# A decoder layer in exact fp32: one projection earlier, the experts' loads between the small transfers, a held piece and one tile's experts later

## The chip, the cores and the metric

The kernel runs on one core of a Trainium2 chip. A core has five engines that run side by side: TensorE (PE: matrix products and transposes, into PSUM), VectorE (DVE), ScalarE (ACT), GpSimd (POOL), and SyncE (SP), which here only issues transfers. The engines work through their own instructions in order and wait for each other through semaphores. Transfers between the chip's memory (HBM) and the core's SBUF are carried out by 16 DMA engines. The metric is the device time of one execution in microseconds (us); lower is better.

## The reference

Sixteen sequences of 128 tokens with 256 features go through one layer of three parts, each followed by "add the input and normalize":

```python
# 1. causal attention, 16 heads of 16, only the 32 largest scores of each row are kept
scores = jnp.einsum('bhqd,bhkd->bhqk', q, k) / math.sqrt(D_HEAD)
scores = jnp.where(causal, neg_inf, scores)
vals, idx = jax.lax.top_k(scores, K_S)                       # K_S = 32
attn = jax.nn.softmax(masked, axis=-1)
x = _layernorm(x + (attn @ v) @ Wo.T + bo)
# 2. eight experts on every token (256 -> 512 -> 256), summed with weights from ctx_512 and itok
h = jax.nn.relu(jnp.einsum('edi,bsi->bsed', proj_in, x))
o = jnp.einsum('eid,bsed->bsei', proj_out, h)
x = _layernorm(x + jnp.einsum('bsei,bse->bsi', o, gate))
# 3. Hadamard transform, 4-bit activations, ternary weights
x = _layernorm(x + jnp.einsum('bsi,oi->bso', xq, wq))
```

All weights and activations of parts 1 and 2 are fp32.

## The kernel before

The 16 sequences form nine tiles of 1, 1, 2, 2, 2, 2, 2, 2 and 2 sequences. Attention works in units: a unit is one tile, one half of the heads (c = 0 or 1) and one sequence. Tiles 0 and 1 have two units each (units 0, 1 and 2, 3), every other tile four.

The engines that compute follow an order written out by hand. One step of the loop `attention()` is one round of VectorE's work on one unit; a unit has STEPS = 9 steps (four rounds of "find the eight largest", L440, and "strike them out", L455, in all). `attn_finish` then ends the softmax: z (L467), its reciprocal (L469), products on VectorE (L471) and POOL (L475). A dictionary `plan`, filled with `at(step, fn, ...)`, says which other function is traced at which step. The functions that matter here:

- `project(u)`: queries and keys of one half of a tile (`queries_keys`, L331). ScalarE writes them from PSUM into qT (L347) and kT (L352). Eight small transfers on SyncE's queue (L365) then spread qT over the block-diagonal buffer qblk. qT comes from a pool with two buffers; a third qT can be written only when the eight transfers of the first have read it. The PSUM tiles of these projections come from the pool psh with two buffers, which the held pieces (L285) and the experts' first product (ph, L618) use too.
- `carry(t)`: values (L375) and the residual.
- `score(u)`: the score products (L396); for units after the first, ScalarE copies them to SBUF (L405).
- `attn_turn` (the transposes pta and ptb, L486 and L487, evacuated by ScalarE as pT, L496), `attn_apply` (pav, L507), `attn_end` (py, L520, then VectorE's r, L523, and the normalization to x1) and the transposes px (L535) of x1 to x1T (L536).
- `hoist()`: projections of the last three tiles (6, 7, 8) done early in nine pieces and parked in HBM; until then their inputs and results occupy the places of experts 5, 6 and 7 in SBUF. In the row `for step in (8, 10, 12, 15, 16, 17, 17, 21, 22)` two pieces stand at step 17.
- `load_experts(es)`: two transfers of 512 KB for each expert, on SyncE's queue. They are traced inside `project`, for experts 0 to 2 behind the eight transfers of (t, c) = (2, 0), and for 3 and 4 behind those of (3, 0), where the constant `hada` follows.

The experts (`experts`, L618 and L585, evacuated by ScalarE as hT, L622, and part, L593) and the third part (`ffn`) fill TensorE between attention's products. `pace(step)` says how much of this work must have been traced by a step: the work of tile t is spread evenly from `begin[t]` to `begin[t + 1]`. `begin` is 23, 50, 84 and 120 for the first four tiles. x tiles come from a pool with three buffers, so the x of tile 3 takes over the buffer of tile 0, which r of tile 0 (L523) reads last.

TensorE, VectorE, ScalarE and GpSimd keep the order in which the code is traced. SyncE's transfers are ordered by the scheduler of the language, which keeps them behind what they depend on.

Of the kernel before, what the change touches and what calls it, by code (L numbers as in the profile page):

```python
# [29 lines left out]
def decoder_kernel(ctx: ExitStack, tc: tile.TileContext, i: dict, out: bass.AP):  # L30
# [6 lines left out]
    NT = len(SIZES)  # L37
# [3 lines left out]
    FIRST_UNITS = DC * SIZES[0]  # L41
# [40 lines left out]
    def load_x(t):  # L82
        x = b3.tile([P, TB, D], F32, tag="x", name=f"x{t}")
        nc.sync.dma_start(x[:, : SIZES[t]], i["x"][tokens(t), :].rearrange("(b p) d -> p b d", p=P))
        return x

    def load(t, q):
        return load_T(t, q), load_x(t)

    def load_gates(t):  # L90
        n, bs = SIZES[t], slice(FIRST[t], FIRST[t] + SIZES[t])
        w = b3.tile([P, TB, S], F32, tag="ctx", name=f"ctx{t}")
        nc.sync.dma_start(w[:, :n], i["ctx_512"][bs].rearrange("b k s -> k b s"))
        k = b3.tile([P, TB, S], I32, tag="tok", name=f"tok{t}")
        nc.sync.dma_start(k[:, :n], i["itok"][bs].rearrange("b k s -> k b s"))
        return w, k
# [29 lines left out]
    FIRST_HELD = E - len(HOISTED)  # L126
# [18 lines left out]
    def load_experts(es):  # L145
        for e in es:
            nc.sync.dma_start(w_in[:, e], i["w_in"][e].rearrange("(c p) d -> p c d", p=P))
            nc.sync.dma_start(w_out[:, e], i["w_out"][e].rearrange("(c p) d -> p c d", p=P))
# [127 lines left out]
    def hoist():  # L276

        for t in HOISTED:
            e = place(t)
            xT = w_in[:, e, :, :T]  # L280
            for c in range(DC):
                pp = psh.tile([P, 2, T], F32, tag="ph", name=f"phq{t}_{c}")
                for j, w in enumerate((wqT, wkT)):
                    for cc in range(DC):
                        nc.tensor.matmul(pp[:, j], w[:, cc, ts(c, P)], xT[:, cc], start=cc == 0, stop=cc == DC - 1)  # L285
                for j, bias in enumerate((bq, bk)):
                    nc.scalar.activation(w_out[:, e, 2 * j + c], pp[:, j], AF.Identity, bias=bias[:, c : c + 1])
                if c == DC - 1:
                    qk_held = dram.tile([P, 2, DC, T], F32, name=f"qk_held{t}")
                    nc.sync.dma_start(qk_held.rearrange("p j c s -> p (j c) s"), w_out[:, e])  # L290
                yield
            pv = pso.tile([P, 512], F32, tag="po", name=f"phv{t}").rearrange("p (b d) -> p b d", b=TB)
            for b in range(TB):
                for c in range(DC):
                    nc.tensor.matmul(pv[:, b], xT[:, c, ts(b, S)], wvT[:, c], start=c == 0, stop=c == DC - 1)  # L295
            nc.scalar.copy(w_in[:, e, :, T:], pv)
            v_held = dram.tile([P, TB, D], F32, name=f"v_held{t}")
            held[t] = qk_held, v_held, nc.sync.dma_start(v_held, w_in[:, e, :, T:])
            yield

    def held_queries_keys(t, c):

        n, src = SIZES[t], held[t][0]
        kT = kTs[(t * DC + c) % len(kTs)]
        qblk = qblks[(t * DC + c + 2) % len(qblks)]
        for g in range(2):
            rows = ts(g, 64)
            nc.sync.dma_start(kT[rows, :, g], src[rows, 1, c].rearrange("p (b s) -> p b s", b=n))
        for h in range(HC):
            ins = nc.sync.dma_start(  # L310
                qblk[ts(h, DH), :, :, h % HG].rearrange("p b m q -> p (b m) q"),
                src[ts(h, DH), 0, c].rearrange("p (m q) -> p m q", q=32),
            )
        return qblk, kT, ins
# [507 lines left out]
    def project(u):  # L822

        if u >= len(units) or units[u][:2] in projected:
            return
        t, c, _ = units[u]
        projected.append((t, c))
        *qk[t, c], ins = held_queries_keys(t, c) if t in HOISTED else queries_keys(t, c, inputs[t][0])
        if c == 0 and 2 < t < NT - 1:
            inputs[t + 1] = (None, load_x(t + 1)) if t + 1 in HOISTED else load(t + 1, nc.sync)  # L830
        if (t, c) in ((2, 0), (3, 0)):
            with tc.issue_after(ins.ins):
                load_experts(range(3) if t == 2 else range(3, FIRST_HELD))
                if t == 3:
                    nc.sync.dma_start(hada, i["hada"][0:P, 0:P])
        if (t, c) == (1, DC - 1):
            gate_inputs[1] = load_gates(1)
# [18 lines left out]
    STEPS = 2 * (TOPK // 8) + 1  # L856
    LAG = 1
    LAST = [DC * sum(SIZES[: t + 1]) - 1 for t in range(NT)]
# [5 lines left out]
    def at(step, fn, *args):  # L864
        plan.setdefault(step, []).append(lambda: fn(*args))
# [25 lines left out]
    for u, (t, c, b) in enumerate(units):  # L891
        s, quick = STEPS * (u + 1), u < FIRST_UNITS
        if (c, b) == (0, 0):
            at(s - STEPS, open_tile, t)
        if u in lag:
            at(s + lag[u], attn_finish, u)
        late = lag.get(u, 0)
        turn = s + (0 if quick else late + 2 if u == LAST[2] else late + 3 if u in lag else 1 if t < 3 else 3)
        at(turn, attn_turn, u)
        at(turn + 2, products, u)  # L900
        if u == LAST[t]:
            for k in (2, 3, 4, 4) if quick else (4, 6, 10, 11) if t == 1 else (6, 8, 10, 11):
                at(s + k, end, t)
            for k in (-3, -1, *range(5, 5 + E)) if quick else (-5, -3, *range(9, 9 + E)):
                at(s + k, next_of_gates, t)
            at(s - 1, next_gates, t + 2)
    for u in range(len(units) - 1):
        at(STEPS * u + (5 if u == FIRST_UNITS else 1), score, u + 1)
    for step, u in ((3, 2), (5, 3), (7, 4), (STEPS + 3, 6), (2 * STEPS + 3, 8)):
        at(step, project, u)  # L910
    for step, t in ((3, 1), (7, 2), (2 * STEPS + 5, 3)):
        at(step, carry, t)
    for u in range(FIRST_UNITS + 1, len(units)):
        at(STEPS * u + 5, project, u + 6)
        if u + 6 < len(units) and units[u + 6][1:] == (0, 0):
            at(STEPS * u + 7, carry, units[u + 6][0])
    for step, zs in ((1, [odd(vms[2]), odd(vms[3])]), (6, [pTs[1], odd(vms[4]), odd(vms[5])])):
        at(step, zeros_later, zs)
    hoisting = hoist()
    for step in (8, 10, 12, 15, 16, 17, 17, 21, 22):  # L920
        at(step, next, hoisting)

    def load_held_experts():
# [6 lines left out]
    for step in (38, 40, 47, 49, 56):  # L930
        at(step, next, weights_of_last)

    begin = [STEPS * (LAST[t] + 1) + (5, 14, 12)[t] if t < 3 else STEPS * (LAST[t] + 1) + 12 for t in range(NT)]

    def attention():
        project(0)
        score(0)
        project(1)
        carry(0)
        inputs[3] = load(3, nc.sync)  # L940
        for u in range(len(units)):
            yield from attn_weights(u, scores.pop(u))
        for _ in range(begin[-1] - STEPS * len(units)):
            yield
# [31 lines left out]
    for step, _ in enumerate(attention()):  # L976
        for fn in plan.get(step, ()):
            fn()
        while done < pace(step):
            c = next(work)  # L980
# [48 lines left out]
```

## Time and profile before

| | us |
|---|---|
| median of 3 runs | 621.82 (621.14 to 622.28) |
| the profiled execution's own time | 622.15 |
| its span, first to last instruction | 620.4 |
| TensorE busy | 599.4 (97%) |
| VectorE busy | 508.6 (82%) |
| ScalarE busy | 339.3 (55%) |
| POOL busy | 303.0 (49%) |
| 16 small transfers of 8 KB on SyncE's queue, issue to landing, median | 1.8 |
| qk and v held transfers, 512 and 256 KB, median | 8.3 and 3.3 |
| expert loads of 512 KB, median (w_in, w_out) | 6.9 and 8.0 |

The granted clock of TensorE was full (0.994 on average), so differences are not due to the clock. In the lines shown below, a group of a timeline gives its start, its length (both us), engine, line, operation, output and inputs, count, and in square brackets the idle time of its engine just before it with what ended that; a wait list gives the sum of waits, their number and the longest. Where the engine named as the releaser had long been done, it was another thing, often a transfer. The time from issue to landing of a transfer is in the view of transfers, which can be narrowed to one issue.

### The profile page before, as it was taken

What the parts mean: (1) busy time and instruction counts of PE and PEld (TensorE: products, weight loads), DVE (VectorE), ACT (ScalarE), POOL (GpSimd) and SP (SyncE); (2) the same over time, 40 slices, a digit from 0 to 9 for tenths busy, and PEclk for the clock granted to TensorE, in tenths of its full rate; (3) what the DMA queues carried; (4) which work ended last, traced back from release to release, by engine and by line L of the source; (5) the groups of instructions that cost most, each with busy time, mean ns of one, the idle gap of its engine ahead of it and who ended that gap; (6) DMA issues with size and microseconds to landing.
All of it is one profiled execution on the core that took longest, in us unless ns stands there. A gap on an engine that the chain in (4) does not pass through costs nothing.

```text
span 620.4 us, 12489 instructions
## 1 busy us (share of the span) xinstructions
PE 599.4 (97%) x3534; PEld 522.4 (84%) x3534; DVE 508.6 (82%) x3132; ACT 339.3 (55%) x1016; POOL 303.0 (49%) x574
## 2 busy tenths in 40 slices
PE   6989999999999999999999999999999999999993
PEld 5779898988888888888888888888888888888882
DVE  6978999989967999889979997899969996431346
ACT  3867667665666565556565655546565655341112
POOL 6204553412883438623883468443772368227013
PEclk9999999999999999999999999999999999999997
DMA  7184940010002100130003000000000000000000
GB/s 239 38 260 141 323 111 6 23 27 8 11 19 38 40 19 2 29 57 3 17 18 52 18 10 1 1 18 1 2 1 1 18 10 2 0 18 1 0 18 17
DMA packets 53589, 25.13 MB, mean 40 GB/s; under 512 B 31888, under 2 KB 51088, under 8 KB 53520
## 3 DMA queue, kind: packets, MB, share of 16 engines
q1 hardware_dynamic: 52960, 24.20, 14.3%
q8 instruction: 28, 0.46, 0.3%
q14 instruction: 41, 0.34, 0.2%
q10 hardware_dynamic: 560, 0.13, 0.1%
HBM read 18.68 MB, written 4.46 MB: 37 GB/s over the span
## 4 chain that ended last, share of the span: by engine, by line
PE 89%; DVE 5%; ACT 4%; issue 1%; POOL 1%; DMA 0%; ACTq 0%; DVEq 0%
PE po L585 34%; PE ph L618 34%; PE ps L396 5%; PE pav L507 3%; PE pqk L331 3%; PE py L520 2%; PE pta L486 2%; PE phq L285 1%; DVE wk L455 1%; ACT ex L431 1%; DVE m L440 1%; PE pv L375 1%; PE phv L295 1%; ACT pT L496 1%; PE ptb L487 1%
## 5 line engine op out<-in xcount | busy, mean ns | idle before, releaser
L618 PE MATMUL ph<-x1T,w_in 128*128 128x256 f32 (+1 forms) x1152 | 237.4, 359 | 2.5 <-ACT hT L622 1.2
L585 PE MATMUL po<-w_out,hT 128*128 128x256 f32 x1024 | 236.3, 380 | 0.0
L618 PEld LDWEIGHTS ph<-x1T,w_in 128*128 128x128 f32 x1152 | 197.7, 190 | 27.2 <-ACT hT L622 1.9
L585 PEld LDWEIGHTS po<-w_out,hT 128*128 128x128 f32 x1024 | 190.7, 190 | 24.9 <-issue 1.0
L622 ACT ACTIVATE hT<-ph 128x512 f32<-128x512 f32 (+1 forms) x144 | 78.7, 549 | 124.3 <-PE ph L618 123.8
L455 DVE MATCH_REPLACE8 wk<-m,wk 128x64 f32<-128x64 f32 (+2 forms) x576 | 132.2, 240 | 0.0
L440 DVE MAX8 m<-wk 128x8 f32<-128x64 f32 (+2 forms) x576 | 100.7, 242 | 0.0
L593 ACT ACTIVATE part<-po,gate 128x256 f32<-128x256 f32 x112 | 52.9, 472 | 76.8 <-PE po L585 75.9
L475 POOL TENSOR_TENSOR wk<-wk,rz 128x128 f32<-128x128 f32 (+2 forms) x92 | 47.7, 543 | 94.1 <-DVE wk L471 94.1
L596 POOL TENSOR_TENSOR acc<-acc,part 128x512 f32<-128x512 f32 (+1 forms) x56 | 65.0, 1160 | 33.9 <-ACT part L593 33.4
L431 ACT ACTIVATE ex<-sc,nb 128x32 f32<-128x32 f32 (+1 forms) x248 | 74.3, 351 | 0.0
L702 POOL TENSOR_TENSOR xh<-xh 128x256 f32<-128x256 f32 x98 | 67.7, 711 | 1.5
L411 POOL TENSOR_TENSOR sc<-sc,cmask 128x64 f32<-128x64 f32 (+1 forms) x93 | 31.8, 370 | 47.3 <-ACT sc L405 47.2
L396 PEld LDWEIGHTS ps<-kT,qblk 128*128 128x128 f32 x256 | 42.4, 195 | 5.6 <-POOL qblk L362 1.4
L455 DVE MATCH_VALUE_LOAD wk<-m,wk 128x8 f32 x576 | 45.0, 78 | 0.0
L396 PE MATMUL ps<-kT,qblk 128*128 128x256 f32 (+3 forms) x256 | 43.4, 313 | 1.3 <-ACT qblk L360 1.0
L455 DVE MATCH_REPLACE8 wk<-m,sc 128x64 f32<-128x64 f32 (+1 forms) x186 | 42.7, 242 | 0.0
L564 DVE SCALAR_TENSOR_TENSOR junk<-wt 128x128 f32<-128x128 f32 x128 | 39.6, 340 | 0.0
L440 DVE MAX8 m<-sc 128x8 f32<-128x32 f32 (+1 forms) x248 | 38.2, 224 | 0.0
L496 ACT COPY pT<-pta 96x256 f32<-96x256 f32 (+2 forms) x96 | 35.1, 366 | 1.3 <-PE pta L486 0.6
L405 ACT COPY sc<-ps 128x512 f32<-128x512 f32 (+1 forms) x62 | 23.3, 428 | 18.1 <-PE ps L396 18.0
L471 DVE SCALAR_TENSOR_TENSOR wk<-wk,ex 128x352 f32<-128x352 f32 x64 | 30.5, 518 | 0.0
(187 smaller groups left out, 634.5 us busy)
## 6 DMA issues: line engine op xcount, KB each, us to landing
w_in<-in_w_in SPq DMA_DIRECT2D x8, 512.0 KB, 6.9
w_out<-in_w_out SPq DMA_DIRECT2D x8, 512.0 KB, 8.0
x<-in_x SPq DMA_DIRECT2D x7, 256.0 KB, 3.1
out_y<-y SPq DMA_DIRECT2D x7, 256.0 KB, 2.1
qk_held<-w_out SPq DMA_DIRECT2D x3, 512.0 KB, 8.3
xT<-in_xT SPq DMA_DIRECT2D x4, 256.0 KB, 3.1
qblk<-qT SPq DMA_DIRECT2D x64, 16.0 KB, 1.9
ctx<-in_ctx SPq DMA_DIRECT2D x7, 128.0 KB, 2.1
```

The source lines that it names most:

```text
L396: ins = nc.tensor.matmul(view(parts[PLACE[0, j] // 512], at, [[step, 2], [1, 32 * (j + 1)]]), qblk[:, b, j].rearrange("p h q -> p (h q)"), ...
L431: nc.scalar.activation(ex[:, keys(m)], sc(m), AF.Exp, bias=nb[:, m : m + 1], scale=SCALE, accum_out=z[:, m : m + 1] if m < 2 else None,)
L440: nc.vector.max(m8[:, m, ts(r, 8)], left(m))
L455: nc.vector.match_replace(wk[:, keys(m)], m8[:, m, ts(r, 8)], left(m), TAKEN)
L475: eng.tensor_tensor(view(wk, at, [[step, 2], [1, size]]), view(src, at, [[step, 2], [1, size]]), rz[:, 2 * j : 2 * j + 2].unsqueeze(2).to_ ...
L496: nc.scalar.copy(pT[0:rows, heads, q : q + 32], src.rearrange("p (h q) -> p h q", q=32))
L585: nc.tensor.matmul(po, hT[:, f, ts(b, S)], w_out[:, e, f], start=f == 0, stop=f == FC - 1)
L593: nc.scalar.activation(part[:, b], po, AF.Copy, scale=gates[t][:, b, e : e + 1])
L596: sums.append(lambda: nc.gpsimd.tensor_tensor(acc[:, :n], (acc if e else x1)[:, :n], part[:, :n], ALU.add))
L618: nc.tensor.matmul(ph[:, f, : n * S], w_in[:, e, c, ts(2 * k + f, P)], x1T[:, c, : n * S], start=c == 0, stop=c == DC - 1,)
L622: ins = nc.scalar.activation(hT[:, ts(k, 2), : n * S], ph[:, :, : n * S], AF.Relu)
L702: nc.gpsimd.tensor_tensor(pairs(xh, c, half), pairs(from_, 0, half), pairs(from_, 1, half), op)
```

## The change

Four edits. `project(2)`, the projections of tile 1's first half, moves from step 3 to step 1 and is traced ahead of `score(1)`. The loads of experts 0 to 2 now follow the small transfers of (1, 0), and those of experts 3 and 4, with `hada`, follow the transfers of (1, 1). One of the held pieces of step 17 moves to step 19, behind the transposes of unit 1's weights. The experts of the third tile begin at step 85 instead of 84.

```diff
@@ project
-        if (t, c) in ((2, 0), (3, 0)):
+        if t == 1:
             with tc.issue_after(ins.ins):
-                load_experts(range(3) if t == 2 else range(3, FIRST_HELD))
-                if t == 3:
+                load_experts(range(3) if c == 0 else range(3, FIRST_HELD))
+                if c:
                     nc.sync.dma_start(hada, i["hada"][0:P, 0:P])
...
+    at(1, project, FIRST_UNITS)
     for u in range(len(units) - 1):
         at(STEPS * u + (5 if u == FIRST_UNITS else 1), score, u + 1)
-    for step, u in ((3, 2), (5, 3), (7, 4), (STEPS + 3, 6), (2 * STEPS + 3, 8)):
+    for step, u in ((5, 3), (7, 4), (STEPS + 3, 6), (2 * STEPS + 3, 8)):
         at(step, project, u)
...
-    for step in (8, 10, 12, 15, 16, 17, 17, 21, 22):
+    for step in (8, 10, 12, 15, 16, 17, 19, 21, 22):
         at(step, next, hoisting)
...
-    begin = [STEPS * (LAST[t] + 1) + (5, 14, 12)[t] if t < 3 else STEPS * (LAST[t] + 1) + 12 for t in range(NT)]
+    begin = [STEPS * (LAST[t] + 1) + (5, 14, 13)[t] if t < 3 else STEPS * (LAST[t] + 1) + 12 for t in range(NT)]
```

`issue_after` only sets the order: the loads go to the queue behind that transfer and do not wait for it to land.

## The prediction

> **What bounds the kernel now.** I read the page first, then the waits of TensorE, then the timelines of TensorE, ScalarE, VectorE and SyncE's queue up to 145 us. Names: (t,c) is half c of tile t; "the eight of (t,c)" are the eight qblk transfers (L365) that read qT(t,c).
>
> ```profile
> span 620.4 us, 12489 instructions
> PE 599.4 (97%) x3534; PEld 522.4 (84%) x3534; DVE 508.6 (82%) x3132; ACT 339.3 (55%) x1016; POOL 303.0 (49%) x574
> ...
> PE pqk L331 <- DMA WqT<-in_WqT: 3.9, 1, 3.9
> PE pav L507 <- ACT pT L496: 2.3, 2, 1.6
> ...
> PE ph L618 <- ACT hT L622: 1.2, 1, 1.2
> PE ps L396 <- ACT qblk L360: 1.0, 1, 1.0
> ...
> PE ph L618 <- ACT x1T L536: 0.7, 1, 0.7
> PE ph L618 <- ACT part L593: 0.6, 1, 0.6
> ```
>
> TensorE is busy 599.4 of 620.4 us. Its waits between the first loads and 139 us are 6.8 us in 10 places; from 139 to 600 us it has none. So any time that TensorE loses or wins before 139 us arrives at the end unchanged: nothing later has room to give it back, and the work is the same in both kernels.
>
> Up to 139 us a second chain runs beside it: VectorE's selection of the largest scores. It is busy 9.9 of each 10 us from 60 to 110 us and never waits for TensorE there. The two meet where TensorE transposes weights (pta, L486), and where VectorE needs py (L520).
>
> ScalarE's waits matter most for this change:
>
> ```profile
> 20.19 0.49 ACT L215 COPY vm<-zero 128x128 f32<-128x128 f32 x2
> 22.76 0.47 ACT L347 ACTIVATE qT<-pqk,bq 128x256 f32<-128x256 f32 x1 [2.08 <-PE ptb L487]
> ```
>
> qT has two buffers, so qT(2,0) can be written only when the eight of (1,0) have landed. The named ptb has nothing to do with it: the last of the eight is issued at about 20.7 us and lands 1.8 us later, 22.5 us, and ScalarE goes on at 22.76. Everything on ScalarE queues behind such a wait.
>
> SyncE's queue shows the next thing, here where four expert matrices are in flight:
>
> ```profile
> 58.11 0.47 SPq L147 DMA_DIRECT2D w_in<-in_w_in  x1
> 58.62 0.47 SPq L148 DMA_DIRECT2D w_out<-in_w_out  x1
> 59.13 0.51 SPq L147 DMA_DIRECT2D w_in<-in_w_in  x1
> ...
> 63.24 0.67 SPq L148 DMA_DIRECT2D w_out<-in_w_out  x1
> 64.56 0.94 SPq L147 DMA_DIRECT2D w_in<-in_w_in  x1
> 66.40 0.85 SPq L148 DMA_DIRECT2D w_out<-in_w_out  x1
> ```
>
> The first three land 4.9, 5.9 and 7.2 us after issue: 63.0, 64.5, 66.3 us. The issues at 63.24, 64.56 and 66.40 are the eighth after each of them. So a transfer on this queue is issued only when the one eight places ahead of it has landed. The same holds from 10 to 15 us (bo lands at 10.2, Wf goes at 10.25).
>
> **The change, part by part.**
>
> *Projections of (1,0) ahead of the second unit's scores.* They fill the 1.01 us in which TensorE waits for qblk L360, and free the 0.35 us wait behind kT. TensorE then stands at the first pta at about 20.5 instead of 21.92 us, but the weights it transposes are ready at 21.83 us as before: VectorE is busy back to back from 9.4 us, and POOL ends last. Gain at that point 0. On ScalarE qT(1,0) moves from 15.59 to 12.35 us, into idle time; the score copies at 13.62 stay.
>
> *The eight of (1,0)* then wait only for the queue (busy to 15.15 us): they start at 15.2 instead of 16.05, end at 20.5, and qT(2,0) is written at 21.9 instead of 22.76. That is worth 0.86 us on ScalarE up to 28.9 us, and pav's 0.70 us wait shrinks to 0.1.
>
> *The experts' loads.* In the built program's order SyncE now issues the eight of (1,0), six expert loads (3.15 MB), the eight of (1,1), four more loads and hada, six of the eight of (2,0), x of tile 3, and the last two of (2,0). Before, all 24 small ones went ahead of any load. The first six loads were issued from 32.68 us; the last two landed so late:
>
> ```profile
> w_in<-in_w_in SPq DMA_DIRECT2D x1, 512.0 KB, 9.4
> w_out<-in_w_out SPq DMA_DIRECT2D x1, 512.0 KB, 10.2
> ```
>
> Issued at 34.89 and 35.47, they landed at 44.3 and 45.7 us: 13.0 us after the first issue. Now the first issue is at 20.5, so the sixth lands at 33.5 us. The eighth of (1,1) is eight places behind it: issued at 33.5, landed after 1.85 us, seen by ScalarE 0.25 us later: qT(2,1) is written at T = 35.6 us, where ScalarE would be there at 28.9 (before: 29.78, unhindered). Queued behind it on ScalarE are kT, a held copy, four ex groups, the exp of d for unit 1, four evacuations and pT.
>
> From T by the spacings of before (qT at 29.78): the exp of d ends T+3.42 = 39.0, VectorE's z of unit 1 starts there (before 33.54), and 7.17 us of VectorE work on, r (L523) at 46.2 (before 42.73). TensorE loses 5 us at phq of tile 7 (its PSUM buffer is kT's, evacuated at T+1.31), but pta of unit 1 would have waited for the weights to T+5.7 = 41.3 anyway.
>
> *Two of (2,0) behind x of tile 3.* x of tile 3 takes over the buffer that r reads; before, it was issued 0.07 us after r's end (43.22). Now two of the eight of (2,0) stand behind it: r ends 46.7, x 46.75, the two at 47.2 and 47.85, landed and seen at 50.0. qT(3,0) can only then be written (before 44.52). From qT(3,0) ScalarE has 2.95 us of work to the ex of unit 2, so 53.0 (before 48.67, held then by TensorE's phv), and the exp of d for unit 2 ends 4.3 us later than before, as does hT of the first expert. VectorE (z at 52.44) and TensorE (second expert's ph at 52.7) both stand waiting for these. Shift: +4.3 us on both chains. It moves 1:1 with T.
>
> Bounds: the 3.15 MB at the quickest row of a 2 us window (396 GB/s) are 8.0 us, with 1.2 us to start and 1.8 to land 11.0 instead of 13.0: +2.3. At 2.55 us for each load, as the four from 58.11 (the last lands 68.3), 15.3: +6.6. I take 13.0, since it is the same six loads from an idle queue.
>
> [...] The rows decide: the queue's stretches with all 16 engines busy move about 340 GB/s.
>
> A small transfer behind loads is slower too: the qblk issued at 43.69, with the last load and a held write still in flight, landed after 4.0 us, those from 16 to 32 us after 1.8 to 1.9. [...]
>
> *Experts 3 and 4 earlier.* ph at 63.13 waits 0.58 us; its w_in was issued at 58.11 and landed at 63.0, so the "ACT part" named is that load. This wait goes. But pta at 69.00 started as VectorE's and POOL's weights came (68.95); TensorE will stand there instead. Gain 0. The loads of experts 5 to 7 land before TensorE needs them (before: 71.7 for use at 73.2; now SyncE reaches them at about 63, with nothing ahead).
>
> *Held piece at step 19 instead of 17.* phq of tile 8 (1.73 us) goes behind pta of unit 1 and fills the 1.55 us wait before pav. It would bring r 1.6 us forward if VectorE were free; VectorE is at r only at 46.2, so 0.
>
> *Third tile's experts a step later* (begin[2]: 84 to 85). Tile 1's experts are spread over 35 steps instead of 34, so pieces fall behind attention's work:
>
> ```profile
> 121.98 1.11 PE L618 MATMUL ph<-x1T,w_in 128*128 128x128 f32 x8
> 122.93 0.64 PE L486 MATMUL pta<-ident,wk 128*128 128x128 f32 x4
> ...
> 135.46 1.95 PE L585 MATMUL po<-w_out,hT 128*128 128x256 f32 x8
> 137.58 0.67 PE L535 MATMUL px<-ident,x 128*128 128x128 f32 x4 [0.17 <-DVE x L269]
> 138.92 1.99 PE L618 MATMUL ph<-x1T,w_in 128*128 128x256 f32 x8 [0.68 <-ACT x1T L536]
> 141.05 0.66 PE L486 MATMUL pta<-ident,wk 128*128 128x128 f32 x4
> ```
>
> In before's times: the ph at 121.98 now follows pta. TensorE is at pta 0.95 us sooner, but POOL's weights come at 122.86: 0.95 us idle, and py and all of VectorE's chain behind it 0.95 us later. The po at 135.46 now follows px. After ps (136.4) nothing is left before px, whose x is ready at 138.5: 2.1 us idle. px and po end at 140.7; pta's weights come at 142.0: 1.3 us idle; the ph of 138.92 follows. TensorE's waits become 4.35 where they were 1.66 (counted from one possible start to the next): +2.7 us. Below: if x came in time, px's 0.85 us of waits would be filled, -0.85. Above: pav, now directly behind pta and two ph, waits for pT as long as its longest wait (1.6): 4.3. I take 2.7, since each of its terms is read off these rows. After 142 us TensorE is 1.7 us further behind VectorE than before, so the later moved pieces find their weights ready: 0.
>
> **Sum.** 4.3 + 2.7 = +7.0 us on the profiled execution: 622.15 (its span 620.4 and 1.75 around it) becomes 629.15. That execution is 0.33 above the median 621.82, so I predict 628.8.
>
> **The rivals.**
> Transfers only (the third tile's step costs nothing): +4.3 - 0.85 = +3.45, 625.3. For it: VectorE may run ahead of TensorE by then. Against: from 69 to 123 us both move together.
> Third tile only (the eight of (1,1) land by 30): +2.7, and down to -1 where ScalarE's 0.86 us and the held piece's gain come through: 623.5 to 624.5. For it: the six loads and the small ones could share the engines. Against: the three issues at 63 to 66 us.
> Longer loads (15.3 us): +9.3, 631.1.
> Faster: the moved pieces fill gaps and nothing new waits. The filled waits are 1.01, 0.35, 0.70, 1.55, 0.58 and 0.85, together 5.0: at best 616.8. It decides only if attention's weights are at each pta when TensorE is, 1 to 1.4 us earlier than before; at 21.83 and 122.86 us the rows say that they are not.
>
> **How the numbers follow.** Both parts 0.62 (626.8 to 631.1 by the loads' bounds), transfers only 0.12, third tile only 0.12, longer loads 0.06, faster 0.06, no change 0.02. Range 624.0 to 631.8. Within 0.2% (1.2 us) is no change that this measurement can tell: 0.03; faster 0.06; slower 0.91.
>
> **What would show it.** ScalarE idle some 6 us before qT(2,1), written near 35.6; VectorE idle about 7 us, not 1.8, before z of unit 1; x of tile 3 issued near 46.7 and qT(3,0) near 50; TensorE idle about 2 us at the third px (near 143) and 1.3 at the pta behind. Wrong if qT(2,1) is written by 30 us, or if px finds its x ready.

## The result, and the profile after

The changed kernel took 629.81 us (median of five runs, 628.48 to 631.29). The kernel before took 621.81 us beside it (five runs, 621.14 to 622.28). The ratio is 1.0127, with a 95% interval of 1.0114 to 1.0139: the change costs 8.0 us. The prediction was 628.8, within 624.0 to 631.8.

The profiled execution of the changed kernel took 628.53 us, near the lower end of its five. Its span grew from 620.4 to 626.8 us. These are the first lines of its page, and the line of the granted clock from the page's second part (40 slices of 15.7 us, in tenths of full speed):

```profile
span 626.8 us, 12492 instructions
PE 601.3 (96%) x3534; PEld 524.1 (84%) x3534; DVE 508.7 (81%) x3132; ACT 338.4 (54%) x1016; POOL 302.4 (48%) x574
...
PEclk9989999998999999999999999999999999999997
```

TensorE is busy 1.9 us longer for the same instructions (599.4 before), and idle 4.5 us longer (25.5 of 626.8, where it was 21.0 of 620.4). The two digits 8 in the clock line, slices three and ten (near 35 and near 142 us), mark two stretches at half speed (a granted clock of 0.50 in the windows of 1 us inside them). The projections of held pieces there (phq) take 1.7 us more in sum, po 1.7 and px 0.3; other groups take 1.7 us less in sum (ps, ph, pav and pqk), the first of them because the start ran faster in this execution. So the clock is a part of the difference here, though it was full in the kernel before (0.994 on average).

TensorE's waits in the changed kernel (sum, number, longest, in us), without those that both kernels have alike:

```profile
PE phq L285 <- ACT kT L352: 3.2, 1, 3.2
PE ph L618 <- ACT hT L622: 2.8, 3, 1.2
PE pta L486 <- POOL wk L422: 2.2, 2, 1.3
...
PE px L535 <- DVE x L269: 1.9, 1, 1.9
...
PE pav L507 <- ACT pT L496: 0.7, 1, 0.7
PE pta L486 <- POOL wk L475: 0.4, 1, 0.4
```

The waits for qblk (1.0), x1T (0.7) and part (0.6) are gone, and pav's 2.3 became 0.7. In their place stand 3.2 us at the held phq, 2.2 and 0.4 us at pta, and 1.9 us at px.

**The first stage.** SyncE's queue in the changed kernel, from the timeline (start, length, both us; x8 is eight transfers):

```profile
20.17 0.58 SPq L147 DMA_DIRECT2D w_in<-in_w_in  x1
...
22.96 0.51 SPq L148 DMA_DIRECT2D w_out<-in_w_out  x1
23.57 8.90 SPq L365 DMA_DIRECT2D qblk<-qT  x8
...
45.49 0.37 SPq L84 DMA_DIRECT2D x<-in_x  x1
45.91 1.23 SPq L365 DMA_DIRECT2D qblk<-qT  x2
```

Eight such transfers took 5.2 us with no load ahead of them (those of (1,0), from 14.89); the eight of (1,1) are issued over 8.9. The sixth load, issued at 22.96, landed 8.9 us later, at 31.86. The eighth small transfer went at 31.89 (first the line of the view of transfers for that load, then the timeline):

```profile
w_out<-in_w_out SPq DMA_DIRECT2D x1, 512.0 KB, 8.9
...
31.89 0.58 SPq L365 DMA_DIRECT2D qblk<-qT  x1
```

ScalarE's writes of qT, with its idle time before each in brackets, show what followed:

```profile
21.60 0.47 ACT L347 ACTIVATE qT<-pqk,bq 128x256 f32<-128x256 f32 x1 [2.31 <-DMA qblk<-qT]
33.81 0.47 ACT L347 ACTIVATE qT<-pqk,bq 128x256 f32<-128x256 f32 x1 [5.08 <-DMA qblk<-qT]
48.64 0.47 ACT L347 ACTIVATE qT<-pqk,bq 128x256 f32<-128x256 f32 x1 [1.88 <-DMA qblk<-qT]
```

These are qT(2,0), qT(2,1) and qT(3,0); before, they were written at 22.76, 29.78 and 44.52. VectorE's z of unit 1, r, and z of unit 2 come behind them:

```profile
37.27 0.35 DVE L467 TENSOR_REDUCE z<-d 128x6 f32<-128x192 f32 x1 [6.22 <-ACT d L448]
45.00 0.42 DVE L523 SCALAR_TENSOR_TENSOR r<-py,x 128x256 f32<-128x256 f32 x1 [0.57 <-PE py L520]
55.22 0.35 DVE L467 TENSOR_REDUCE z<-d 128x6 f32<-128x192 f32 x1 [2.37 <-ACT d L448]
```

Before, they stood at 33.54, 42.73 and 52.44 us.

TensorE's timeline shows something that the prediction did not have: the products behind the wait run at half speed.

```profile
30.92 1.03 PE L285 MATMUL phq<-w_in,WkT 128*128 128x256 f32 x4
35.17 2.07 PE L285 MATMUL phq<-w_in,WqT 128*128 128x256 f32 x4 [3.23 <-ACT kT L352]
37.04 1.81 PE L285 MATMUL phq<-w_in,WkT 128*128 128x256 f32 x4
```

The same four products take 1.03 us at 30.92 and 2.07 us at 35.17. Windows of 1 us say why. Their columns are the window and its length, the busy time and instructions of PE, PEld, DVE, ACT and POOL, the granted clock, the DMA share and GB/s; the clock is the third figure from the right:

```profile
35.00:36.00 1.00, 0.82 (x2) 0.74 (x3) 0.00 (x0) 0.95 (x3) 0.00 (x0) 0.60 1.05 389
36.00:37.00 1.00, 1.00 (x3) 0.76 (x3) 0.00 (x0) 1.00 (x5) 0.00 (x0) 0.50 1.06 376
37.00:38.00 1.00, 1.00 (x4) 0.77 (x3) 0.70 (x3) 0.95 (x3) 0.00 (x0) 0.50 0.87 232
38.00:39.00 1.00, 1.00 (x6) 0.75 (x5) 1.00 (x4) 0.11 (x1) 0.34 (x1) 0.69 0.97 349
```

**The second stage.** TensorE around the third px, in the changed kernel:

```profile
125.38 0.66 PE L486 MATMUL pta<-ident,wk 128*128 128x128 f32 x4 [0.43 <-POOL wk L475]
...
140.93 1.02 PE L535 MATMUL px<-ident,x 128*128 128x128 f32 x4 [1.95 <-DVE x L269]
141.75 3.22 PE L585 MATMUL po<-w_out,hT 128*128 128x256 f32 x8
144.81 0.60 PE L486 MATMUL pta<-ident,wk 128*128 128x128 f32 x4
...
151.89 1.99 PE L618 MATMUL ph<-x1T,w_in 128*128 128x256 f32 x8 [1.16 <-ACT hT L622]
```

px waits 1.95 us for its x, as the moved po is now behind it. That po takes 3.22 us, not 1.89: the clock is halved here too (0.50 in the windows from 142 to 144 us). The wait at 151.89 was not foreseen either.

Where the 6.4 us of span arise: at the pta of unit 3 (before, then changed) 2.8 are there, and 3.5 if the start is allowed for, which was 0.76 us quicker in this execution (first pta at 21.16, before 21.92). The other 3.6 come between 105 and 155 us.

```profile
69.00 0.66 PE L486 MATMUL pta<-ident,wk 128*128 128x128 f32 x4
...
71.76 0.66 PE L486 MATMUL pta<-ident,wk 128*128 128x128 f32 x4 [0.92 <-POOL wk L422]
```

### The profile page after: what moved, and what is told of

It reads as the page before. It is cut to its first block, busy times and chain, and to the rows that moved or that the text cites. A ratio compares the mean times of both kernels' runs of the same rounds, so it can differ in the third digit from the quotient of the medians.

```text
span 626.8 us, 12492 instructions
## 1 busy us (share of the span) xinstructions
PE 601.3 (96%) x3534; PEld 524.1 (84%) x3534; DVE 508.7 (81%) x3132; ACT 338.4 (54%) x1016; POOL 302.4 (48%) x574
## 4 chain that ended last, share of the span: by engine, by line
PE 78%; DVE 15%; DMA 2%; ACT 2%; SPq 1%; issue 1%; POOL 1%; ACTq 0%; DVEq 0%
PE po L585 31%; PE ph L618 31%; DVE wk L455 5%; PE ps L396 4%; DVE m L440 4%; PE pav L507 2%; PE py L520 2%; PE pta L486 2%; DMA w_out<-in_w_out 1%; PE pqk L331 1%; DVE junk L564 1%; DVE wk L471 1%; PE phq L285 1%; SPq L365 1%; DMA qblk<-qT 1%
## 5 line engine op out<-in xcount | busy, mean ns | idle before, releaser
L467 DVE TENSOR_REDUCE z<-d 128x6 f32<-128x192 f32 x32 | 11.1, 346 | 30.0 <-ACT d L448 30.0
```

## The experiments

The table lists all of them (there is no e6), each beside runs of the kernel before that were measured together with it. "As before" and "changed" say where the loads stand; the column of the third tile gives the step at which its experts begin. In e4, e8, e11, e12 and e13 added lines raise the later line numbers by 3 to 10; the names of the tiles are the same.

| run | loads | third tile | projection, held piece | other | median (range; runs), us | against before | ratio (95%) |
|---|---|---|---|---|---|---|---|
| changed kernel | changed | 85 | changed | | 629.81 (628.48 to 631.29; 5) | +8.00 | 1.0127 (1.0114 to 1.0139) |
| e1 | as before | 85 | changed | | 623.16 (622.6 to 623.8; 11) | +1.23 | 1.0020 (1.0011 to 1.0028) |
| e2 | changed | 84 | changed | | 626.69 (624.79 to 628.02; 6) | +4.76 | 1.0077 (1.0061 to 1.0093) |
| e3 | as before | 84 | changed | | 619.39 (619.22 to 620.02; 5) | -2.54 | 0.9959 (0.9947 to 0.9971) |
| e8 | changed | 85 | changed | TensorE kept busy | 628.89 (628.51 to 629.53; 4) | +6.96 | 1.0111 (1.0098 to 1.0125) |
| e4 | changed | 85 | changed | place for qT(2,1) | 623.42 (623.21 to 623.98; 9) | +1.24 | 1.0024 (1.0015 to 1.0034) |
| e7 | 4 and 6 | 85 | changed | | 630.03 (629.4 to 630.42; 4) | +7.85 | 1.0130 (1.0116 to 1.0144) |
| e9 | as before | 84 | projection only | | 621.10 (620.7 to 621.62; 11) | -1.08 | 0.9986 (0.9977 to 0.9995) |
| e10 | as before | 83 | changed | | 620.39 (619.7 to 621.8; 11) | -1.79 | 0.9975 (0.9966 to 0.9984) |
| e5 | changed | 84 | as before | | 628.53 (626.75 to 628.64; 5) | +5.80 | 1.0089 (1.0074 to 1.0103) |
| e11 | as before | 84 | changed | place for qT(2,0) | 618.77 (618.52 to 619.19; 5) | -3.96 | 0.9941 (0.9929 to 0.9954) |
| e12 | changed | 84 | changed | place for qT(2,0) | 618.78 (618.32 to 619.08; 5) | -3.95 | 0.9941 (0.9928 to 0.9953) |
| e13 | changed | 84 | changed | as e12, early products | 618.63 (618.29 to 618.82; 5) | -3.13 | 0.9945 (0.9932 to 0.9959) |

The medians of before that go with them were 621.81 (changed kernel), 621.93 (e1, e2, e3, e8), 622.18 (e4, e7, e9, e10), 622.73 (e5, e11, e12) and 621.76 (e13).

### One part put back at a time

e1 puts the loads back:

```diff
-        if t == 1:
+        if (t, c) in ((2, 0), (3, 0)):
             with tc.issue_after(ins.ins):
-                load_experts(range(3) if c == 0 else range(3, FIRST_HELD))
-                if c:
+                load_experts(range(3) if t == 2 else range(3, FIRST_HELD))
+                if t == 3:
```

> The changed kernel with the experts' loads back behind the transfers of (2,0) and (3,0); the earlier projection, the held piece at step 19 and the third tile's later begin stay. My theory (the eight places of SyncE's queue make qT(2,1) late): qT(2,1) is written at about 29 us, not 33.8; the 5.1 us wait of ScalarE there, the 3.2 us wait of TensorE at phq and the slowly running phq behind it (2.07 and 1.81 us, where such a group takes 1.03) are gone; time 625.5 to 626.5, 3.5 to 4.3 below the changed kernel's 629.8. Rival 1 (loads cost nothing, all of the loss is the third tile's): 629 to 630. Rival 2 (all of the loss is the loads'): 621.5 to 622.5.

Measured: 623.16 us, 6.65 below the changed kernel. qT(2,1) is written at 29.38 us, the wait at phq and the slow phq are gone (the clock is 1.00 from 35 to 39 us). More came back than expected (3.5 to 4.3), so a part of the loads' cost had been missing from the account.

e2 puts the third tile back:

```diff
-    begin = [STEPS * (LAST[t] + 1) + (5, 14, 13)[t] if t < 3 else STEPS * (LAST[t] + 1) + 12 for t in range(NT)]
+    begin = [STEPS * (LAST[t] + 1) + (5, 14, 12)[t] if t < 3 else STEPS * (LAST[t] + 1) + 12 for t in range(NT)]
```

> The changed kernel with the third tile's experts beginning at step 84 again, and all else as changed. My theory: the third px finds its x ready (wait 0.2, not 1.95 us), its po runs at 1.9 and not 3.2 us, ph near 152 us doesn't wait 1.16 us for hT; time 625.8 to 626.8, 3 to 4 us below the changed kernel's; the first 60 us stay as in the changed kernel. Rival 1 (third tile's step costs nothing): 629 to 630. Rival 2 (the lateness of the first 72 us alone makes px wait, whatever the step): px waits 1 to 2 us still, 628.5 to 630.

Measured: 626.69 us, 3.1 below the changed kernel. px waits 0.16 us, its po takes 1.95 us, not 3.22, and no ph waits near 152 us; the first 60 us look as in the changed kernel, after a start 0.6 us later. So px's wait comes from the step, not from the lateness of the first stage.

e3 puts both back:

> The changed kernel with both undone: only the earlier projection of (1,0) and the held piece at step 19 are left. My theory (these two are worth nothing, or a little): 620.5 to 622.0, no more than 0.2% from the kernel before; the first pta at about 21.2 us as in the changed kernel, the pta of 69 us where it was or up to 0.7 us earlier. Rival (the earlier projection or the held piece costs by itself): 623 or more. Rival (the filled waits come through): 619 or less.

Measured: 619.39 us, 2.54 below the kernel before, ratio 0.9959 (0.9947 to 0.9971). No version of the expectation fits but that of the filled waits, and even that one said 619 or less. The two edits that the prediction had costed at nothing are a gain. TensorE in this kernel:

```profile
36.33 0.60 PE L486 MATMUL pta<-ident,wk 128*128 128x128 f32 x4
...
36.88 1.03 PE L285 MATMUL phq<-w_in,WqT 128*128 128x256 f32 x4
37.74 1.03 PE L285 MATMUL phq<-w_in,WkT 128*128 128x256 f32 x4
38.70 0.65 PE L507 MATMUL pav<-pT,vm 128*32 128x128 f32 x16
```

The held piece fills the stretch in which pav waited 1.55 us for pT, and pta goes 2.0 us earlier (38.35 before). VectorE's r follows at 40.69, 2.04 us earlier.

From these four and before, in the differences against before: the loads cost 6.8 us (changed kernel less e1) or 7.3 (e2 less e3), the third tile's step 3.2 (changed kernel less e2) or 3.8 (e1 less e3). The parts nearly add up: -2.5, +7.3 and +3.8 make 8.6 where 8.0 were measured.

### Which of the two small edits gains

e9 is the kernel before with the projection alone:

```diff
+    at(1, project, FIRST_UNITS)
     for u in range(len(units) - 1):
...
-    for step, u in ((3, 2), (5, 3), (7, 4), (STEPS + 3, 6), (2 * STEPS + 3, 8)):
+    for step, u in ((5, 3), (7, 4), (STEPS + 3, 6), (2 * STEPS + 3, 8)):
```

> The kernel before with one edit alone: project(2) at step 1, ahead of the second unit's scores. Loads, held piece (step 17) and third tile as before. It tells which of the two edits carries the 2.5 us that both gain with the loads and the third tile put back (619.39 against 621.93). My theory (the first pta waits for VectorE's chain anyway; the held piece filled the wait ahead of pav): 621.2 to 622.2, and the held piece carries it. Rival (the projection carries it): 619.2 to 620.3. Both a part: between.

Measured: 621.10, 1.08 below before: a part each. VectorE's idle time before z of unit 1 is 0.78 us instead of 1.76, since ScalarE writes qT(2,0) and all behind it a microsecond earlier (21.65 instead of 22.76). How much earlier differs between executions: in e3, with the same projection edit, SyncE reached the eight of (1,0) at 15.77 us instead of 14.95, and qT(2,0) came at 22.48. By the medians the rest of e3's gain, some 1.5 us, is the held piece's.

### The loads alone, and how they cost

e5 is the kernel before with the loads edit alone. It has all eight of (2,0) ahead of x of tile 3, so the second late write should not be there:

> The kernel before with the experts' loads edit alone. In this kernel all eight of (2,0) stand ahead of x of tile 3 on SyncE's queue, so the second late write of qT (by x of tile 3) should not be there, and only the first one is: qT(2,1) near 34.5 us. Theory that the first late write shifts r and all behind it by itself: r near 46, qT(3,0) 1.8 us behind r as in the kernel before, 625 to 626. Rival, after the four-load kernel (only the second late write, that of qT(3,0), costs): 622 to 623. Rival (the loads' edit costs as much without the other edits as with them): 626.5 or more.

Measured: 628.53 us, 5.80 above before, more than the 625 to 626 expected. The reading that only the second write costs is out; the number lies where the last rival put it (as much without the other edits as with them: e2 has 4.76). qT(2,1) came at 35.47, and VectorE then waits for TensorE, not the other way round:

```profile
38.92 0.35 DVE L467 TENSOR_REDUCE z<-d 128x6 f32<-128x192 f32 x1 [7.89 <-ACT d L448]
49.22 0.42 DVE L523 SCALAR_TENSOR_TENSOR r<-py,x 128x256 f32<-128x256 f32 x1 [3.13 <-PE py L520]
```

r comes 10.3 us behind z, not 7.7 as in the changed kernel. TensorE, itself late by 4.5 us of waiting at phq and slowed behind it (2.08 and 1.91 us for phq), here has both held pieces ahead of pta (at 44.83 us; before 38.35). The held piece at step 19 spares the changed kernel this.

e7 leaves four loads ahead of (1,1) instead of six:

```diff
-                load_experts(range(3) if c == 0 else range(3, FIRST_HELD))
+                load_experts(range(2) if c == 0 else range(2, FIRST_HELD))
```

> The changed kernel with four loads (experts 0 and 1) instead of six ahead of the transfers of (1,1), and the other six behind them. The eighth of (1,1) then stands eight places behind the fourth load, which landed near 29 us. Theory of the eight places: qT(2,1) at about 31, not 33.8, TensorE's wait at phq under 1 us and phq at full speed. In this kernel six of (2,0) stand behind x of tile 3, so qT(3,0) comes at about 48.5 as in the changed kernel. If the first late write is what costs (one shift that is carried on): 626 to 627.5. If the second late write (qT(3,0), and by it the exp of d of unit 2) sets the end, so that the first one lies beside it: 629 to 630. Rival (a transfer on this queue does not wait for the one eight places ahead): qT(2,1) stays at 33.8.

The first part came as the eight places have it. The fourth load was issued at 21.95, and the eighth of (1,1), eight places behind it and at the end of this row, at 29.47:

```profile
21.95 0.47 SPq L148 DMA_DIRECT2D w_out<-in_w_out  x1
22.52 7.54 SPq L365 DMA_DIRECT2D qblk<-qT  x8
```

qT(2,1) came at 31.41, 2.4 us earlier than in the changed kernel, TensorE waited 0.72 us at phq, and phq ran at full speed (1.13 us). But the time stayed at 630.03, because six of (2,0) now stand behind x of tile 3:

```profile
31.41 0.47 ACT L347 ACTIVATE qT<-pqk,bq 128x256 f32<-128x256 f32 x1 [2.57 <-DMA qblk<-qT]
49.42 0.47 ACT L347 ACTIVATE qT<-pqk,bq 128x256 f32<-128x256 f32 x1 [5.72 <-PE pv L375]
```

ScalarE stands 5.72 us before qT(3,0) (the named pv had long been done), and TensorE 2.97 us behind it at pv. So taking one late write away can leave the loss as it was: e7 has little of the first, but a larger second (5.72 us where the changed kernel has 1.88). e5 has the first only and loses 5.80, but without the two small edits, so what the first alone costs beside them was not measured.

e4 removes both. qT(2,1) is put into a place that is free then, so it does not wait for the transfers of (1,1), and qT(3,0) then waits for (1,1) and not (2,0):

```diff
-            qT = b2.tile([P, TB, S], F32, tag="qT", name=f"qT{t}_{c}")
+            if (t, c) == (2, 1):
+                qT = tmp("qT2_1", "xh").rearrange("p b d -> p (b d)")[:, : TB * S].rearrange("p (b s) -> p b s", b=TB)
+            else:
+                qT = b2.tile([P, TB, S], F32, tag="qT", name=f"qT{t}_{c}")
```

> The changed kernel, loads and third tile as changed, but qT(2,1) gets a place of its own, so that it does not wait for the transfers of (1,1), and qT(3,0) then waits for those of (1,1), which are done long before. The loads stay in their place and move the same bytes at the same time. My theory (the loads cost only by making these two writes of qT wait): qT(2,1) at about 29 us, qT(3,0) at about 43, no wait of TensorE at phq, no half clock there; 623.0 to 624.0, as with the loads put back (623.16). Rival (the loads' traffic or the held transfers behind them cost by themselves): 626 or more. Rival (the loads cost by another way): 629 to 630.

Measured: 623.42 us, ratio to before 1.0024, where e1, with the loads put back, has 1.0020. qT(2,1) at 28.90, qT(3,0) at 41.89. The loads still go from 20.45 us and the eight of (1,1) still take 9.4 us to issue, and it costs nothing that can be told from e1. So all that the loads cost goes through the two writes of qT behind them; e11 and e12, further down, show the same between two kernels that both give qT(2,0) a place of its own.

### Half speed

e8 fills TensorE's two waits with useless products; 12 and 8 of them:

```diff
+    def warm(name, n):
+        for k in range(4):
+            d = psum(f"{name}{k}")
+            for _ in range(n):
+                nc.tensor.matmul(d, ident16, mask16[0], start=True, stop=True)
...
+                if (t, c) == (HOISTED[1], 1):
+                    warm("wa", 3)
...
+        if t == 2:
+            warm("wb", 2)
```

> The changed kernel with useless bf16 products (128x512, results never read) put into TensorE's two waits: twelve ahead of phq of tile 7 and eight ahead of the third px. It adds work that computes nothing; the output stays. Theory (the granted clock halves after a wait of 2 to 3 us, and phq, phk and po behind it then run at half speed): phq takes about 1.0 and not 2.07 us, po 1.9 and not 3.2 us, the clock stays above 0.9 at 35 to 39 us and 141 to 145 us; gain up to 1.8 us at the first place and 1.3 at the second, less what the pta behind then waits: 627.5 to 629. Rival (phq and po are slow for another reason, such as shared memory or a transfer, not the clock): they stay slow, 629.5 to 631. Rival (the halved clock lies beside other waits and costs nothing): groups at full speed, time within 0.5 us of 629.8.

Measured: 628.89 us, 0.9 below the changed kernel. The clock stays up in both places: 1.00 in the windows from 35 to 39 us, and a 9 in every slice of the page's clock line around px. phq takes 1.13 us, and pta of unit 1 starts 5.8 us after qT(2,1) (35.27 to 41.05), where it was 6.8 in the changed kernel: 1.0 us that the halved clock had cost there. Of it 0.5 us are left at the pta of unit 3 (37.5 us after qT(2,1) in e8, 38.0 in the changed kernel), since VectorE's r, which waits 0.57 us for py in the changed kernel, does not wait in e8 and is set by VectorE itself. The medians differ by 0.9 us, but the two ranges overlap, and of the profiled executions that of e8 is the longer one (629.53 and 628.53). At px it is another matter:

```profile
141.93 0.67 PE L545 MATMUL px<-ident,x 128*128 128x128 f32 x4 [0.22 <-DVE x L269]
142.44 1.89 PE L595 MATMUL po<-w_out,hT 128*128 128x256 f32 x8
145.40 0.66 PE L494 MATMUL pta<-ident,wk 128*128 128x128 f32 x4 [1.07 <-POOL wk L483]
```

po is done in 1.89 us instead of 3.22, and TensorE then waits 1.07 us for POOL's weights at the next pta. In e4 the same came about by itself: its px waited 1.95 us as in the changed kernel, but the clock stayed up.

```profile
135.58 0.67 PE L538 MATMUL px<-ident,x 128*128 128x128 f32 x4 [1.95 <-DVE x L269]
136.09 1.89 PE L588 MATMUL po<-w_out,hT 128*128 128x256 f32 x8
139.06 0.66 PE L489 MATMUL pta<-ident,wk 128*128 128x128 f32 x4 [1.07 <-POOL wk L478]
```

So the halved clock cost 1.0 us at the first pta behind it, of which the rows show 0.5 further on. At the second place it took up a wait that would have been there: the ph that waits for hT starts 11.0 us after px in the changed kernel (151.89) as in e8 (152.90).

### The step the other way

e10 is e3 with the third tile at step 83.

> The earlier projection and the held piece at step 19, loads back, and the third tile's experts beginning at step 83: one step the other way from 84 (85 in the changed kernel). My theory (beginning later makes the second tile's pieces fall behind attention's products, beginning earlier does the opposite): no wait at px or ahead of pta at 121 to 145 us beyond those with 84; 618.5 to 620.0 where 84 has 619.39. Rival (any other step than 84 is worse, since the fit of the pieces between attention's products is a matter of chance): 621 or more.

Measured: 620.39, 1.0 above e3 by the medians, 0.75 by the differences against before. The expectation that earlier is no worse falls: px waits 1.06 us at 83 as well, where it waits 0.17 at 84. The other reading, 621 or more, is not met either. In the rows, this kernel is 0.45 us ahead of e3 at the pta of unit 3 (66.50 against 66.95), and 0.75 behind it at px (136.26 against 135.51). The timelines show where the 1.2 us go. Ahead of the pta at 112.15 and at 121.31 us stands a group of ph that step 84 has behind it. What delays px is another such group, ahead of py:

```profile
126.87 1.05 PE L618 MATMUL ph<-x1T,w_in 128*128 128x128 f32 x8
127.77 1.89 PE L520 MATMUL py<-WoT,oT 128*128 128x256 f32 x8
```

In e3 py starts at 127.01, ahead of that ph. The group takes 0.9 us, and pav ahead of it 0.35 us longer (1.43 instead of 1.08); VectorE's r follows 0.75 us later (129.69 instead of 128.94) and so does px. Both sides of 84 are worse by the medians, but the intervals of e10 and e3 overlap (0.9966 and 0.9971), so the smaller of the two losses is not sure.

### A version that beats both

e11 is e3 with qT(2,0) in a place of its own, with the diff of e4 for `(2, 0)`.

> The earlier projection and the held piece at step 19, loads and third tile as in the kernel before, and qT(2,0) in a place of its own, so that it waits for no transfers (it waited 2 to 3 us at 22 us). Theory (ScalarE then makes pT of the first unit and the exp of d of unit 1 earlier, and the 0.7 us wait ahead of pav and up to 2 us of VectorE ahead of z of unit 1 shrink): 618.3 to 619.0, against 619.39 without. Rival (TensorE's order sets that stage, so nothing comes through): 619.2 to 619.8.

Measured: 618.77 us. qT(2,0) is written at 20.20 us instead of 22.48, VectorE waits 0.42 us before z of unit 1 (1.98 in e3), and pav does not wait.

e12 has the same place for qT(2,0) and the loads early:

> The changed kernel with the third tile's experts beginning at step 84 again and qT(2,0) in a place of its own: qT(2,1) then waits for the transfers of (1,0) and qT(3,0) for those of (1,1), both done long before. The loads stay early. Theory (early loads cost nothing once no write of qT waits behind them): 618.3 to 619.8, the same as with the loads put back. Rival (early loads have another cost): 620.5 or more. Rival (early loads bring something, such as the 0.6 us wait near 63 us): below 618.5.

Measured: 618.78 us, ratio to before 0.9941 (0.9928 to 0.9953). Early loads neither cost nor bring anything here. What they bring and where it goes can be read in two rows. In e11, with the loads as before, TensorE waits for a load:

```profile
60.50 1.13 PE L621 MATMUL ph<-x1T,w_in 128*128 128x128 f32 x8 [1.14 <-DMA w_in<-in_w_in]
```

In e12 that wait is gone, and this one stands 5 us behind it:

```profile
65.84 0.65 PE L489 MATMUL pta<-ident,wk 128*128 128x128 f32 x4 [0.94 <-POOL wk L425]
```

### The clock at the start

In the profiled executions TensorE's first products run at about half speed (in the changed kernel a pqk takes 1.22 us at 3.70 us and 0.61 at 10.29), and the change to full speed comes at differing times, 7.4 to 12.9 us by the durations. The last run starts fourteen useless products at 1 us, on e12:

```diff
+    dull = const.tile([P, P], BF16, name="dull")
+    nc.vector.memset(dull, 0.0)
...
+    start = psum("start")
+    for _ in range(14):
+        nc.tensor.matmul(start[:, :P], dull, dull, start=True, stop=True)
```

> The kernel of the run before it (qT(2,0) in a place of its own, loads early, third tile at step 84), with fourteen useless bf16 products (128x128) on TensorE from about 1 us, while it waits for the first weights until 3.7 us; the output stays. In the profiled executions TensorE's first products run at half speed, and it reaches full speed at a moment that differs from run to run: between 7.5 and 13 us, though the instructions are the same. Theory (full speed comes some microseconds after TensorE's first work, so starting earlier brings it forward): full speed by 6 to 10 us, the first pta half a microsecond earlier, 617.9 to 618.6 against 618.78, and less spread between runs. Rival (the moment has nothing to do with when TensorE starts, or VectorE's chain hides it): 618.5 to 619.1.

Measured: 618.63 us, which cannot be told from e12's 618.78 (the intervals of the ratios overlap), and full speed came at about 10.9 us, worked out from the durations. The theory is not borne out. The first products ran from 1.07 to 2.74 us, and TensorE then waited 1.2 us. Whether products without that gap would do more was not tried.

## Why the prediction was right, and where its steps were not

The time was predicted within about 1 us and the mechanism of the loads holds. The sum came out partly for other reasons than its terms say. In the rows of the profiled execution the first stage cost 3.5 us (start allowed for) where the sum has 4.3, and the second 3.6 where it has 2.7; that these two errors cancel to 7.1 against 7.0 is luck.

- **The experts' loads (predicted +4.3, with the two small edits at 0).** The mechanism is shown by e4, e7 and e12. In the numbers: the sixth load landed 11.7 us after the first issue, not 13.0, so the eighth small transfer went at 31.89, not 33.5, and qT(2,1) was written at 33.81, not 35.6. In the profiled executions of e2, e8 and e5 the same six loads took about 12.1, 12.3 and 12.8 us, by the issue of the eighth small transfer behind them, so the term differs from one execution to the next. Of the 1.8 us, 0.3 are that the first load went at 20.17, not 20.5. z of unit 1 followed at 37.27 (39.0), r at 45.00 (46.2), x of tile 3 at 45.49 (46.7), qT(3,0) at 48.64 (50.0). What failed is the sum's composition. Loads, projection and held piece together are e2's +4.76, close to +4.3. But added to the two edits the loads cost 7.3 (e2 against e3), and alone on the kernel before 5.8 (e5). The two edits, priced at 0, bring 2.5 without the early loads (e3) and about 1 with them (e2 against e5).
- **TensorE at phq ("loses 5 us", hidden by pta's wait for the weights to T + 5.7).** It waited 3.2 us there. With the clock kept up, pta stood at T + 5.8 and waited 0.48 us for POOL's weights (e8), as the step has it; with the halved clock TensorE was the later one, at T + 6.8. The missed term is the halved clock: 1.0 us at this pta, 0.5 at the pta of unit 3.
- **Projection earlier (0 at the first pta).** That pta did wait, 1.32 us in the changed kernel. The 0.86 us that ScalarE gains beside it were named but not summed; alone they are worth 1.1 us (e9).
- **Held piece at step 19 (0, since VectorE is not at r).** Wrong as a price. The 46.2 us for r assumed that TensorE's py is ready by then, and it is so only with this piece moved: in e5, without it, VectorE waits 3.13 us for py. With the loads as before, the piece is worth about 1.5 us (e3 against e9).
- **Two of (2,0) behind x of tile 3 (contained in the +4.3).** qT(3,0) waited 1.88 us for them. The step took it as one shift with the first write. e7 shows that the second can make up for the first, and the loss goes only when both go (e4).
- **Experts 3 and 4 earlier (0, the 0.58 us move to pta).** Borne out: the pta of unit 3 at 71.76 us waits 0.92 us, and the ph waits no longer. e11 and e12 show the same exchange at equal times.
- **Third tile a step later (+2.7).** Measured 3.2 to 3.8. The first pta waits 0.43 us, not 0.95; px 1.95, close to 2.1. The next pta's 1.3 us appear as 1.07 where the clock stays up (e4, e8), and are filled by the slow po where it does not. Not in the sum was the 1.16 us wait at 151.89 for hT: ScalarE has the exp of d, which waits for VectorE's d until 150.99, ahead of that hT. In the kernel before the ph that needs this hT did not yet stand there.
- **Rivals.** "Transfers only" (625.3) and "third tile only" (623.5 to 624.5) fall, since both parts cost; e2 and e1, which have one part each, came 1.4 above the one and 0.3 below the other. "Faster" falls for the changed kernel; its idea, that filled waits come through, is e3, and goes further with e11 (3.96 us below before).

What stays open: the medians differ by 8.0 us, the profiled executions by 6.4. The kernels with the halved clock at 35 us have the wide ranges (2.8 us for the changed kernel, 3.2 for e2, 1.9 for e5). Most of the others range over 0.5 to 1.2 us, but e10 and the kernel before, which have no halved clock there, over up to 2.1. The mean granted clock of each execution points to the halving: the three of e2 below 627 us have 0.991 and 0.992, the three above 0.989; the two of the changed kernel above 631 us have 0.986 and 0.987, the others 0.988 to 0.991. But its two at 628.5 have 0.991 and 0.988, so the clock is not all of it, and as one execution of each kernel was profiled, the cause of the spread stays open.

## What to carry to other kernels

Before a large transfer is moved ahead of small ones, look for who waits for the small ones to be read, and how many places of the queue lie between (the small transfer eight places behind the sixth load went at 31.89 us, as that load landed at 31.86): here two waits of ScalarE for a buffer cost 7 us, and one more buffer made the same loads free. A part that is costed at nothing because another engine is later should be costed once more without that other part; here two such edits were a gain of 2.5 us without the early loads, and of about 1 with them. Moving the schedule of the filler pieces by a single step cost 3.2 to 3.8 us one way and about 0.8 the other (less sure), since a piece that stands behind a product leaves that product's wait empty and a piece ahead of it delays it; so both directions are worth trying.

## What the runs showed of the hardware

**TensorE's clock halved at short waits, but not at all of them.** In the changed kernel it fell from 1.00 to 0.50 for 3.4 us at the wait of 3.23 us (35.2 to 38.6 us), and for 3.4 us again at the wait of 1.95 us at px (141.0 to 144.4 us). Worked out from the windows and the durations behind them, it was halved for about 3.4 us at a wait of 3.61 us (e2) and for about 6.8 us at one of 4.47 (e5). It was not at 2.97 us (e7, at 52.39 us: pv took 1.13 us there). The wait of 1.95 us at px came with a slow po in the changed kernel and e7 (3.22 us in both) and not in e4 (1.89 us), with the same products on both sides of it. The halving began 1.7 us before the end of the wait in e5, within 0.1 us of the end in the changed kernel at both places, and only behind px, which took 0.67 us, in e7. So the length of the wait does not decide alone.

**The start differs between executions.** The first group of score products takes from 1.73 to 2.61 us, and the next projection from 0.66 to 1.17, with the same instructions ahead of them (but for e13's useless ones). In the changed kernel:

```profile
6.60 2.04 PE L396 MATMUL ps<-kT,qblk 128*128 128x256 f32 x8 [0.29 <-ACT kT L352]
8.48 0.66 PE L331 MATMUL pqk<-xT,WqT 128*128 128x128 f32 x4
```

In e12:

```profile
6.60 2.61 PE L399 MATMUL ps<-kT,qblk 128*128 128x256 f32 x8 [0.30 <-ACT kT L355]
9.00 1.17 PE L331 MATMUL pqk<-xT,WqT 128*128 128x128 f32 x4
```

Worked out from where the durations change, full speed came at about 7.4 us in e4, 8 in the changed kernel and 12.9 in e12, all with the first product at 3.7. Single executions are therefore compared from the first pta on, as above, and not from the start of the span. The granted clock shows 1.00 in all windows of 1 us from 3 to 11 us of the changed kernel; only the durations tell it.

**Small transfers behind large ones.** The nine small transfers in the view of 20 to 34 us of the changed kernel (the eight of (1,1) and the last of (1,0)) landed after 5.4 us in the median, where such transfers took 1.8 before; in e4, where the eight of (1,1) took 9.4 us to issue and no write of qT was held up by them, this had no price that can be told from e1 (623.42 and 623.16 us).
